# A tridiagonalisation's next row: spread by a transfer and updated in place of a product on TensorE

## The chip, the cores and the metric

The kernel runs on one core of a Trainium2 chip. The metric is the device time of one execution in microseconds (us), the median of three runs. TensorE is called PE in the profile, VectorE DVE, ScalarE ACT, GpSimd POOL and SyncE SP.

## What is computed

The reference passes x (128 graphs of 64 nodes with 256 features, float32) through four graph layers that share one 64 x 64 adjacency matrix:

```python
h = jnp.maximum(_layernorm(x, axis=-1), 0.0)
x = x + _L0_gnn_ref(h, adj, ...)   # two graph products, then LSTMs over windows of 1 to 4 nodes
h = jnp.maximum(_layernorm(x, axis=-1), 0.0)
x = x + _L1_gnn_ref(h, adj, adj, ...)   # Laplacian filter (largest eigenvalue), attention, MLP
h = jnp.maximum(_layernorm(x, axis=-1), 0.0)
x = x + _L2_gnn_ref(h, adj, ...)   # graph attention
h = jnp.maximum(_layernorm(x, axis=-1), 0.0)
x = x + _L3_gnn_ref(h, adj, ...)   # spectral layer
```

The spectral layer needs all eigenvectors of a 64 x 64 symmetric matrix:

```python
L_norm = d_inv_sqrt[:, None] * L * d_inv_sqrt[None, :]
_, U = jnp.linalg.eigh(L_norm)
agg = jnp.einsum('mn,bnd->bmd', U.T, features)
```

The eigenvectors depend on the adjacency matrix alone, so they are found once, while layer 0 runs on the graphs.

## The kernel before

Nothing is issued as it is written. `gnn_kernel` builds a `Plan`, whose proxies for the engines (`V`, `G`, `PE`, `ACT`, `SP`) only record each operation with what it depends on. `Plan.cost` (line 170) gives each one a cost and a latency from a table, `Plan.schedule` (line 221) fills each engine's queue greedily in order of the modelled time, and `Plan.issue` (line 325) writes the queues out. So each engine's order is fixed before the run, and an instruction that is not ready holds up all that stand behind it on its engine. Every instruction is issued from line 331, which is therefore the only line that the profile shows; the groups are told apart by tiles and shapes.

Operations belong to groups. Groups 0 to 7 are layer 0 on an eighth of the graphs each, whose LSTM steps are long runs of float32 matmuls with 256, 336 and 512 columns. Layers 1 to 3 follow in 16 groups of half that size. The eigen solver is a group of its own, `EIG`. `Plan.rank` (line 317) puts its matmuls first and its operations on other engines last among those that can start; a matmul of `EIG` is planned 0.12 us later than the modelled end of what it needs (`slack`). When `EIG` is done, six more buffers of the arena are free for the layers.

`eig_decomp` reduces the matrix to a tridiagonal one with Householder reflections (lines 429 to 485), finds the eigenvalues by bisection, then the vectors, and takes them back with the accumulated reflections. `AQ` (64 x 128) holds the matrix on its left and the accumulated transformation on its right. Every partition keeps its own copy of the row and of the reflection, so that later steps need no spreading. Step k of the reduction does this:

- the row product (line 435): a matmul whose weights are one column of the identity, broadcast, puts row k of the matrix on all partitions, in a PSUM bank (r);
- the reflection: ScalarE squares the row (439), GpSimd takes the root (441), VectorE copies and corrects it to v (443 to 455), and picks each partition's own entry, vc (459);
- the product p (461): a matmul of vc with `AQ`, again on all partitions;
- the row nw (478), its own entry nwc (481), and the rank-2 update of `AQ` by way of a temporary `up` (483 to 485).

The next row product waits for this update. Two more row products after the loop fetch the last diagonal entries.

The lines in the middle of the chain, in short:

```python
PE.matmul(rf[:, :N], idf[:, k:k1].to_broadcast([P, P]), Af, start=True, stop=True)
...
PE.matmul(pf[:, :2 * N], vcf.to_broadcast([P, P]), AQf, start=True, stop=True)
...
V.scalar_tensor_tensor(nw, p, nt, cv, op0=ALU.mult, op1=ALU.add)
```

SyncE's queue carries all transfers but five: the loads of weights and of x, two stores of 1 MB each (`put`) that move the first two eighths of x out after layer 0, their reloads, and the results.

Of the kernel before, what the change touches and what calls it, by code (L numbers as in the profile page):

```python
# [8 lines left out]
ALU = mybir.AluOpType  # L9
# [3 lines left out]
N = 64  # L13
KS = 7
NSWEEP = 9
NEIG = 4080
EPS = 2.0 ** -24

# [315 lines left out]
def eig_decomp(plan, room, adj, adjT, ident, idf, ones):  # L334
# [10 lines left out]

    V, G, PE, ACT = (plan.proxy(e) for e in ("V", "G", "PE", "ACT"))
    kept = {}
    inner = Carver(room.cut(NEIG))  # L350

    def scope():
        inner.reset([0])
        return inner
# [4 lines left out]
    def W(shape, name, bufs=None):  # L359

        if bufs is None:
            bufs = 2 if shape[-1] < N or name == "lab" else 1
        ring = kept.setdefault((name, tuple(shape)), [])
        if len(ring) < bufs:
            ring.append(room.tile(shape))
        else:
            ring.append(ring.pop(0))
        return ring[-1]

    def F(n, name):  # L370

        if name not in kept:
            kept[name] = room.tile([P, n])
            G.memset(kept[name], 0.0)
        return kept[name]

    def PS():
        return plan.value("bank")
# [17 lines left out]
    AQ = AQf[:N]  # L396
# [23 lines left out]
    Af = AQf[:, :N]  # L420
# [3 lines left out]
    V.memset(E[:, N - 1:N], 0.0)  # L424
    ph = scope()
    vb = [ph.tile([N, 2 * N]) for i in range(2)]
    for v in vb:
        G.memset(v, 0.0)
    for k in range(N - 2):
        v = vb[k % 2]  # L430
        k1 = k + 1
        if k >= 2:
            G.memset(v[:, k - 1:k1], 0.0)
        rf = PS()
        PE.matmul(rf[:, :N], idf[:, k:k1].to_broadcast([P, P]), Af, start=True, stop=True)
        r = rf[:N]
        jk = W([N, N], 'junk')
        n2 = W([N, 1], 'n2')
        ACT.activation(jk[:, :N - k1], r[:, k1:N], AF.Square, accum_out=n2)
        s = W([N, 1], 's')  # L440
        G.tensor_tensor(s, n2, half, op=ALU.pow)
        ACT.copy(D[:, k:k1], r[:, k:k1])
        V.tensor_copy(v[:, k1 + 1:N], r[:, k1 + 1:N])
        am = W([N, 1], 'am')
        V.tensor_reduce(am, r[:, k1 + 1:N], op=ALU.max, axis=AX.X, apply_absolute_value=True)
        al = W([N, 1], 'al')
        V.tensor_copy(al, r[:, k1:k1 + 1])
        g = W([N, 1], 'g')
        V.tensor_scalar(g, al, 0.0, -2.0, op0=ALU.is_ge, op1=ALU.mult)
        V.tensor_scalar(am, am, 0.0, None, op0=ALU.is_gt)  # L450
        nz = W([N, 1], 'nz')
        V.scalar_tensor_tensor(nz, n2, 1e-36, am, op0=ALU.is_gt, op1=ALU.mult)
        be = W([N, 1], 'be')
        V.scalar_tensor_tensor(be, g, 1.0, s, op0=ALU.add, op1=ALU.mult)
        V.tensor_sub(v[:, k1:k1 + 1], al, be)
        vcf = F(1, f'vc{k % 2}')
        vc = vcf[:N]
        jk2 = W([N, N], 'junk2')
        V.scalar_tensor_tensor(jk2, v[:, :N], 1.0, ident, op0=ALU.mult, op1=ALU.mult, accum_out=vc)
        pf = PS()  # L460
        PE.matmul(pf[:, :2 * N], vcf.to_broadcast([P, P]), AQf, start=True, stop=True)
        p = pf[:N, :2 * N]
        t1 = W([N, 1], 't1')
        V.scalar_tensor_tensor(t1, al, be, n2, op0=ALU.mult, op1=ALU.subtract)
        V.tensor_scalar(t1, t1, -1e-36, None, op0=ALU.min)
        nt = W([N, 1], 'nt')
        V.reciprocal(nt, t1)
        V.tensor_mul(nt, nt, nz)
        V.scalar_tensor_tensor(E[:, k:k1], v[:, k1:k1 + 1], nz, al, op0=ALU.mult, op1=ALU.subtract, reverse1=True)
        pv = W([N, 1], 'pv')  # L470
        jk3 = W([N, N], 'junk3')
        V.scalar_tensor_tensor(jk3, p[:, :N], 1.0, v[:, :N], op0=ALU.mult, op1=ALU.mult, accum_out=pv)
        c2 = W([N, 1], 'c2')
        V.tensor_scalar(c2, pv, nt, nt, op0=ALU.mult, op1=ALU.mult)
        cv = W([N, 2 * N], 'cv')
        V.tensor_scalar(cv, v, c2, 0.5, op0=ALU.mult, op1=ALU.mult)
        nw = W([N, 2 * N], 'nw')
        V.scalar_tensor_tensor(nw, p, nt, cv, op0=ALU.mult, op1=ALU.add)
        nwc = W([N, 1], 'nwc')
        jk2 = W([N, N], 'junk2')  # L480
        V.scalar_tensor_tensor(jk2, nw[:, :N], 1.0, ident, op0=ALU.mult, op1=ALU.mult, accum_out=nwc)
        up = W([N, 2 * N], 'up')
        V.tensor_scalar(up, nw, vc, None, op0=ALU.mult)
        V.scalar_tensor_tensor(up[:, :N], v[:, :N], nwc, up[:, :N], op0=ALU.mult, op1=ALU.add)
        V.tensor_add(AQ, AQ, up)
    rf = PS()
    PE.matmul(rf[:, :N], idf[:, N - 2:N - 1].to_broadcast([P, P]), Af, start=True, stop=True)
    PE.matmul(rf[:, N:2 * N], idf[:, N - 1:N].to_broadcast([P, P]), Af, start=True, stop=True)
    r = rf[:N]
# [19 lines left out]
    k1 = W([N, N], 'k1')  # L509
# [96 lines left out]
    ph = scope()  # L606
# [3 lines left out]
    SG = ph.tile([N, N + 1, C])  # L610
    for s_ in range(NSWEEP):
        V.tensor_scalar(w, w, 1.0 / (KS + 1), None, op0=ALU.mult)
# [35 lines left out]
    ph = scope()  # L648
# [216 lines left out]
P = 128  # L865
# [46 lines left out]
def gnn_kernel(ctx: ExitStack, tc: tile.TileContext, a, out):  # L912
# [153 lines left out]
    room = Carver(arena)  # L1066

    QT, Vc, inner = eig_decomp(plan, room, adj2[:N], adjT2[:N], ident[:N, :N], ident, ones)
    for dst, lhs, rhs in ((Ublk, QT, Vc), (UTblk, Vc, QT)):
        l2 = inner.tile([P, 2, N])  # L1070
# [491 lines left out]
```

## Time and profile before

| what | value |
|---|---|
| median of 3 runs | 2227.12 us (2226.85 to 2229.72) |
| span of the profiled execution | 2226.0 us |
| PE busy | 2192.1 us, 98% |
| DVE busy | 1682.7 us, 76% |
| ACT busy | 971.0 us, 44% |
| POOL busy | 561.0 us, 25% |
| granted TensorE clock | 0.997 |

The first part of the page gives each engine's busy time and number of instructions. The second cuts the span into 40 slices of 55.65 us and gives the busy share of each in tenths. A busy PE is not PE at its peak, since the matmuls overlap: the distance between the starts of two matmuls tells what one costs. A group's line ends with the idle time of its engine just ahead of it. The list of transfers gives the median time from issue to landing.

### The profile page before, as it was taken

The page shows a single profiled execution, that of the slowest core. Times are in us where ns is not written, and L with a number is a line of the kernel's source. Part 1 is how long each engine was busy: PE and PEld are TensorE (multiplying, and loading weights), DVE is VectorE, ACT ScalarE, POOL GpSimd, SP SyncE. Part 2 cuts the span into 40 slices and gives each one's busy share as a digit, 9 for nine tenths or more (in the row PEclk, how much of TensorE's full clock was granted, in tenths as well). Part 3 has the DMA queues.
Part 4 walks back from the last instruction along what each step waited for, and adds up shares of the span by engine and source line. Part 5 has one row for each costly group of instructions (what it writes and reads, how often), then busy time and mean ns, then how long its engine had stood idle before and what let it go on. Part 6 is the DMA issues. An engine that isn't in the chain of part 4 may idle for free.

```text
span 2226.0 us, 42054 instructions
## 1 busy us (share of the span) xinstructions
PE 2192.1 (98%) x15540; PEld 1507.5 (68%) x15540; DVE 1682.7 (76%) x6966; ACT 971.0 (44%) x1945; POOL 561.0 (25%) x856
## 2 busy tenths in 40 slices
PE   9999999999999999999999999999999999999997
PEld 6568468568558657657647756777777777676776
DVE  7667665755799999999998943467777878776697
ACT  4233343333333333333233343256456566545674
POOL 3101100200100100100100302345545456554353
PEclk9999999999999999999999999999999999999999
DMA  7000000100000000000000011000000000000001
GB/s 256 0 1 20 0 1 1 58 1 1 1 1 1 1 1 1 1 1 1 6 1 1 1 46 33 1 2 1 20 2 20 30 12 30 11 21 1 2 2 58
DMA packets 27694, 36.03 MB, mean 16 GB/s; under 512 B 3552, under 2 KB 24928, under 8 KB 26976
## 3 DMA queue, kind: packets, MB, share of 16 engines
q1 hardware_dynamic: 26384, 32.29, 4.4%
q8 instruction: 122, 2.00, 0.4%
q10 hardware_dynamic: 1104, 1.05, 0.2%
q14 instruction: 84, 0.69, 0.1%
HBM read 22.85 MB, written 10.49 MB: 15 GB/s over the span
## 4 chain that ended last, share of the span: by engine, by line
PE 88%; DVE 8%; ACT 2%; POOL 1%; issue 1%; DMA 0%; SPq 0%; DVEq 0%; ACTq 0%
PE bank L331 88%; DVE arena L331 3%; DVE stat L331 1%; DVE big L331 1%; DVE x L331 1%; DVE mids L331 1%; POOL stat L331 1%; ACT arena L331 1%; ACT mids L331 1%; POOL big L331 0%; ACT big L331 0%; ACT L331 0%; DMA adj<-in_adj_dram 0%; DVE Whh L331 0%; ACT x L331 0%
## 5 line engine op out<-in xcount | busy, mean ns | idle before, releaser
L331 PE MATMUL bank<-big,Wih 128*128 128x256 f32 (+2 forms) x2576 | 859.3, 476 | 5.5 <-ACT big L331 2.1
L331 PEld LDWEIGHTS bank<-big,Wih 128*128 128x128 f32 x2576 | 478.2, 190 | 274.0 <-issue 160.1
L331 ACT ACTIVATE mids<-bank,bl 128x256 f32<-128x256 f32 (+2 forms) x624 | 344.3, 562 | 623.7 <-PE bank L331 615.7
L331 PE MATMUL bank<-big,Whh 128*128 128x256 f32 (+3 forms) x1752 | 505.3, 429 | 0.0
L331 DVE TENSOR_TENSOR arena<-arena 64x21 f32<-64x21 f32 (+6 forms) x2312 | 372.3, 192 | 35.3 <-POOL arena L331 1.7
L331 PEld LDWEIGHTS bank<-big,Whh 128*128 128x128 f32 (+1 forms) x1752 | 306.5, 186 | 132.9 <-issue 66.7
L331 DVE TENSOR_TENSOR big<-big,mids 128x256 f32<-128x256 f32 (+2 forms) x192 | 96.7, 504 | 141.1 <-ACT mids L331 139.8
L331 DVE TENSOR_TENSOR big<-mids 128x512 f32<-128x512 f32 (+2 forms) x256 | 143.3, 563 | 37.6 <-ACT mids L331 34.4
L331 POOL TENSOR_SCALAR stat<-stat 128x4 f32<-128x4 f32 (+1 forms) x228 | 62.6, 275 | 390.3 <-DVE stat L331 377.6
L331 ACT ACTIVATE mids<-big 128x256 f32<-128x256 f32 (+2 forms) x176 | 89.8, 510 | 97.6 <-DVE big L331 68.8
L331 DVE TENSOR_SCALAR arena<-arena 64x1 f32<-64x1 f32 (+5 forms) x596 | 119.2, 208 | 8.9 <-POOL arena L331 0.7
L331 POOL TENSOR_TENSOR big<-big,B1T 128x512 f32<-128x512 f32 x32 | 36.0, 1133 | 349.6 <-DVE big L331 184.6
L331 POOL TENSOR_TENSOR stat<-stat,mhalf 128x4 f32<-128x4 f32 (+1 forms) x114 | 120.4, 1057 | 6.8
L331 POOL TENSOR_TENSOR arena<-arena 64x1 f32<-64x1 f32 x66 | 42.4, 643 | 301.1 <-DVE arena L331 155.4
L331 ACT ACTIVATE mids<-x,stat 128x256 f32<-128x256 f32 x96 | 50.7, 591 | 97.2 <-POOL stat L331 97.1
L331 DVE SCALAR_TENSOR_TENSOR arena<-arena 64x1 f32<-64x1 f32 (+4 forms) x391 | 79.8, 211 | 12.7 <-POOL arena L331 5.5
L331 PE MATMUL bank<-Wih,big 128*128 128x256 f32 (+1 forms) x384 | 87.9, 365 | 0.0
L331 DVE BATCH_NORM_STATS2 stat<-x 128x6 f32<-128x256 f32 x240 | 87.7, 409 | 0.0
L331 PE MATMUL bank<-Whh,big 128*128 128x256 f32 (+1 forms) x400 | 85.4, 357 | 1.9 <-ACT big L331 1.2
L331 POOL MEMSET arena<- 64x2 f32 (+5 forms) x72 | 7.9, 112 | 306.8 <-DVE arena L331 306.8
L331 ACT COPY big<-bank 128x512 f32<-128x512 f32 x86 | 47.2, 585 | 66.2 <-PE bank L331 63.6
L331 PEld LDWEIGHTS bank<-Whh,big 128*128 128x128 f32 (+1 forms) x400 | 62.2, 181 | 19.6 <-issue 7.5
(338 smaller groups left out, 3326.0 us busy)
## 6 DMA issues: line engine op xcount, KB each, us to landing
x<-in_x_dram SPq DMA_DIRECT2D x7, 1024.0 KB, 13.7
out_dram<-x SPq DMA_DIRECT2D x24, 256.0 KB, 2.3
Wih<-in_WihT_dram SPq DMA_DIRECT2D x3, 1024.0 KB, 15.9
Whh<-in_WhhT_dram SPq DMA_DIRECT2D x3, 1024.0 KB, 12.0
put<-x SPq DMA_DIRECT2D x2, 1024.0 KB, 4.4
arena<-put SPq DMA_DIRECT2D x2, 1024.0 KB, 5.1
out_dram<-arena SPq DMA_DIRECT2D x8, 256.0 KB, 2.2
Whh<-in_W_dram SPq DMA_DIRECT2D x2, 512.0 KB, 3.9
```

The lines of the kernel that those rows point to most:

```text
L331: getattr(self.engines[op.eng], name)(*map(real, args), **{k: real(a) for k, a in kw.items()})
```

## The change

From step `KROW` = 6 on there is no row product. Row k + 1 of the old matrix is sent from its partition to all 64 partitions by a transfer at the start of step k (`rb`), while the reflection of step k is computed. When nw is known, two operations on VectorE add the step's update of that row to the copies (`rn`), and step k + 1 reads its row from there, from SBUF. The row does so ahead of the update of `AQ`, which it no longer waits for. The update of `AQ` itself is written as two operations in place, without the temporary. The aim is to take one matmul and its waits out of every step.

```diff
+KROW = 6
...
-    V, G, PE, ACT = (plan.proxy(e) for e in ("V", "G", "PE", "ACT"))
+    V, G, PE, ACT, SP = (plan.proxy(e) for e in ("V", "G", "PE", "ACT", "SP"))
...
     vb = [ph.tile([N, 2 * N]) for i in range(2)]
+    rbs, rns = ([ph.tile([N, N]) for i in range(2)] for j in range(2))
...
-        rf = PS()
-        PE.matmul(rf[:, :N], idf[:, k:k1].to_broadcast([P, P]), Af, start=True, stop=True)
-        r = rf[:N]
+        if k < KROW:
+            rf = PS()
+            PE.matmul(rf[:, :N], idf[:, k:k1].to_broadcast([P, P]), Af, start=True, stop=True)
+            r = rf[:N]
+        else:
+            r = rn
+
+        if k + 1 >= KROW:
+            rb = rbs[k % 2]
+            SP.dma_start(rb[:, k1:], AQ[k1:k1 + 1, k1:N].unsqueeze(1).to_broadcast([1, N, N - k1]))
...
-        up = W([N, 2 * N], 'up')
-        V.tensor_scalar(up, nw, vc, None, op0=ALU.mult)
-        V.scalar_tensor_tensor(up[:, :N], v[:, :N], nwc, up[:, :N], op0=ALU.mult, op1=ALU.add)
-        V.tensor_add(AQ, AQ, up)
+        if k + 1 >= KROW:
+            rn = rns[k % 2]
+            V.scalar_tensor_tensor(rn[:, k1:], nw[:, k1:N], v[:, k1:k1 + 1], rb[:, k1:], op0=ALU.mult, op1=ALU.add)
+            V.scalar_tensor_tensor(rn[:, k1:], v[:, k1:N], nw[:, k1:k1 + 1], rn[:, k1:], op0=ALU.mult, op1=ALU.add)
+        V.scalar_tensor_tensor(AQ, nw, vc, AQ, op0=ALU.mult, op1=ALU.add)
+        V.scalar_tensor_tensor(AQ[:, :N], v[:, :N], nwc, AQ[:, :N], op0=ALU.mult, op1=ALU.add)
```

The built program has 56 matmuls fewer and 57 transfers more on SyncE's queue, and the planner's order changes on every engine.

## The prediction

> **What bounds the kernel now.** I read the page's first two parts, then the chain, then TensorE's own groups and its order of time around one step of the tridiagonalisation, and last the transfers.
>
> ```profile
> PE 2192.1 (98%) x15540; PEld 1507.5 (68%) x15540; DVE 1682.7 (76%) x6966; ACT 971.0 (44%) x1945; POOL 561.0 (25%) x856
> ...
> PE   9999999999999999999999999999999999999997
> ...
> DVE  7667665755799999999998943467777878776697
> ...
> PE 88%; DVE 8%; ACT 2%; POOL 1%; issue 1%; DMA 0%; SPq 0%; DVEq 0%; ACTq 0%
> ```
>
> TensorE is busy in all 40 slices but the last, and the chain that ended last is 88% TensorE. VectorE fills up (slices 13 to 22) only in the bisection. The tridiagonalisation runs from 35 to 604 us, by the first and last row product in the timeline. Windows of it and of the bisection:
>
> ```profile
> 100.00:600.00 500.00, 496.78 (x2540) 335.94 (x2539) 324.79 (x1663) 182.98 (x486) 64.05 (x144) 1.00 0.03 9
> 600.00:1230.00 630.00, 625.77 (x2935) 407.10 (x2934) 580.29 (x2887) 218.69 (x425) 24.97 (x36) 1.00 0.00 1
> ```
>
> The columns are length, then TensorE, weight loads, VectorE, ScalarE, GpSimd. Where the change acts, TensorE has 3.2 us idle in 500 and VectorE is 65% busy. So the eigen chain does not set the time. It is fill-in work, and it costs TensorE the matmuls that it puts between those of layer 0. These are the product p (first line) and the row product (second line, 64 of them, two instructions each):
>
> ```profile
> L331 PE MATMUL bank<-arena 128*128 128x128 f32 x124 | 23.8, 274 | 0.0
> ...
> L331 PE MATMUL bank<-arena,ident 128*128 128x64 f32 x128 | 21.5, 251 | 0.0
> ```
>
> Their last column says that TensorE never idled ahead of them: in the planned order both are ready when their turn comes. What one row product costs is not its 251 ns but how far it pushes the matmuls behind it:
>
> ```profile
> 302.00 1.86 PE L331 MATMUL bank<-big,Wih 128*128 128x336 f32 x6
> 303.70 1.86 PE L331 MATMUL bank<-big,Whh 128*128 128x336 f32 x6
> 305.39 0.33 PE L331 MATMUL bank<-arena,ident 128*128 128x64 f32 x2
> 305.56 0.79 PE L331 MATMUL bank<-big,Whh 128*128 128x336 f32 x2
> 306.18 0.73 PE L331 MATMUL bank<-big,Wih 128*128 128x336 f32 x2
> ```
>
> A 336-column matmul takes (303.70 - 302.00) / 3 = 0.567 us when nothing is between. From the row product's start to the second start behind it, one such matmul included, are 306.18 - 305.39 = 0.79 us. So a row product costs 0.79 - 0.567 = 0.223 us of the bounding engine.
>
> **What the Trainium skill says.** "Perfetto Trace Analysis", section "Identifying the Most-Contended Engine", warns that busy time of matmuls is no measure of distance to the limit because they are pipelined; that is why I price by spacing. The trace agrees: two instructions of 251 ns move the stream by only 223 ns. "DMA: Bandwidth & Descriptors", section "Anatomy of one DMA — SWDGE (gpsimd) path", gives about 2.0 us fixed and bytes / 436e9 on top (for the GpSimd path; ours is SyncE's). The trace's small SyncE transfers land after 2.0 to 2.5 us, which agrees. The same page, "Queues, rings and completion order", says that each DMA engine consumes a ring's descriptors in order; so a row sent behind a 1 MB store waits for it. No row of before shows that.
>
> **The change, part by part.**
>
> *Removed from TensorE:* the row products of steps 6 to 61, 62 - 6 = 56 of them (the built programs hold 8058 and 8002 matmuls). 56 x 0.223 = 12.5 us. Nothing hides it, since the matmuls behind close up.
>
> *Moved:* r is now read from SBUF instead of PSUM, and is made from the copy of the row before the update of AQ instead of after it. The step that this shortens, from the timeline:
>
> ```profile
> 168.18 0.20 ACT L331 ACTIVATE arena<-bank 64x48 f32<-64x48 f32 x1 [0.18 <-PE bank L331]
> ...
> 170.56 0.38 PE L331 MATMUL bank<-arena 128*128 128x128 f32 x2
> ...
> 171.89 0.34 DVE L331 SCALAR_TENSOR_TENSOR arena<-bank,arena 64x128 f32<-64x128 f32 x1
> ...
> 172.41 0.27 DVE L331 TENSOR_SCALAR arena<-arena 64x128 f32<-64x128 f32 x1
> 172.72 0.28 DVE L331 SCALAR_TENSOR_TENSOR arena<-arena 64x64 f32<-64x64 f32 x1
> 173.03 0.28 DVE L331 TENSOR_TENSOR arena<-arena 64x128 f32<-64x128 f32 x1
> ...
> 173.81 0.33 PE L331 MATMUL bank<-arena,ident 128*128 128x64 f32 x2
> ```
>
> From p (170.56) to the end of nw (171.89 + 0.34 = 172.23) are 1.67 us; from the square (168.18) to p 2.38 us; between nw and the next square stood the three updates, the row product and its waking, 173.81 + (168.18 - 167.75, its own row product's start) - 172.23 = 2.0 us. After the change, between nw and the square stand nwc's issue (0.15), two row updates with one AQ update between them (0.27 each after the 64x64 row, the pipelined middle about 0.2) and a wake (0.1): about 1.0 us. The step becomes 1.67 + 1.0 + 2.38 = 5.05 us at most. It may be 4.6 us, since the copies that here alternate with ScalarE on the bank (the idle 0.27 and 0.22 us on VectorE at 168.72 and 169.25) need no turns in SBUF. This shortens a chain that does not bound, so I take nothing for it. The bisection starts and ends earlier, under a TensorE that is full either way.
>
> *On VectorE:* out go tensor_scalar, scalar_tensor_tensor and add (0.27 + 0.28 + 0.28 = 0.83 us), in come four scalar_tensor_tensor (0.34 as the nearest 64x128 one, 0.27, 0.27, 0.27: 1.15 us). 0.3 x 56 = 17 us more on an engine with 175 us idle in this window: hidden.
>
> *Added:* 57 row transfers on SyncE's queue. Nearest rows:
>
> ```profile
> put<-x SPq DMA_DIRECT2D x2, 1024.0 KB, 4.4
> ...
> Whh<-in_L_b_dram SPq DMA_DIRECT2D x1, 64.0 KB, 3.2
> ...
> Whh<-in_g_dram SPq DMA_DIRECT2D x1, 1.0 KB, 2.3
> ```
>
> The last has 256 pieces of 4 bytes; ours has 64 of 8 to 232 bytes. The middle one spreads one row over 128 partitions. So a landing between 2.0 (the skill's fixed part) and 3.2 us; I take 2.4.
>
> *The added wait:* the first row update waits for the landing. Behind it on VectorE, in order, stand the AQ updates and layer 0's gate products; behind those ScalarE's tanh, and p on TensorE, which blocks everything behind it. How much time there is comes from the built program's TensorE order, priced with the trace's spacings (0.43, 0.567 and 0.857 us for 256, 336 and 512 columns, 0.223 us for 64 and 128). Between two p the work was at least 6.05 us before, and is at least 4.96 us after, 5.3 to 5.9 us in most tight steps. From the row update's start to the end of the AQ updates I count 1.0 us, so a landing may take 4.96 - 1.0 = 4.0 us before anything waits. At 2.4, or even 3.2, it is hidden. And a step of 5.05 us against these spacings costs less than 1 us in all (five steps lie below 5.0).
>
> Two rows stand behind the two 1 MB stores in SyncE's order (4.4 us). Each could be late by up to 4.4 + 2.4 - 4.0 = 2.8 us, bounds 0 and 5.6 us together. The planner puts long steps around the stores, so I take 0.
>
> Sum: 2227.1 - 12.5 = 2214.6 us.
>
> **The rivals.**
>
> *A, the stream closes up:* 2214.6 us, give or take 4 us, because the planner recasts the whole order (about 34 us of idle TensorE are spread over the start, the change of layers near 1085 to 1450 us and the last 66 us, where 11.2 are idle). Chance 0.72.
>
> *B, the idle places grow:* the reordered tail, the two stores, or p waiting by some tenths in tight steps give back 8 us: 2222.6 us. Against it: no idle ahead of p now. For it: the tail is decided by near ties in the planner. Chance 0.13.
>
> *C, the idle places shrink:* the eigen solver ends earlier, and its arena becomes buffers for the next layers earlier, which takes some 7 us out of the idle near 1085 to 1450 us: 2207.6 us. Chance 0.08.
>
> *D, the transfer takes the place of the row product:* if a landing took 6 us, a step could not be shorter than 7.0 us, and adding what the steps below that lack gives 40 us: 2214.6 + 40 = 2254 us, slower than before. It breaks even near 5 us (steps of 6.05 us lack 12.7 us). Against it are landings of 2.0 to 3.2 us for small transfers. For it: a row from one SBUF partition to 64 is nowhere in this trace. A VectorE that waits in line would look the same. Chance 0.07.
>
> **How the numbers follow.** The likeliest is A. 2208 to 2223 holds nearly all of A, and half of B and of C: about 0.8. Faster by over 0.2% means below 2222.7 us: A, C and nearly a third of B, 0.84. B's rest gives 0.09 for no change, D 0.07 for slower.
>
> **What would show it.** TensorE's busy time falls by some 10 to 13 us and its idle stays near 34 us. The group of 64-column products with ident shrinks from 128 to 16 instructions. The group of p keeps 0.0 idle ahead of it. Row transfers land in about 2.4 us. The last p comes near 485 us instead of 600 us. I am wrong if VectorE's row update waits for the DMA by a microsecond in most steps, if idle appears ahead of p, or if idle in the last 70 us or at the change of layers moves by more than 5 us.

## The result, and the profile after

The changed kernel took 2206.98 us (2205.22 to 2207.11) beside 2227.37 us (2226.85 to 2229.72) for the kernel before: 20.4 us less, ratio 0.9905, 95% interval 0.9887 to 0.9922. Both times are medians of four runs. The prediction was 2214.6 us with a range of 2208 to 2223. The direction was right, the size was 7.6 us short, and the result lies just below the stated range.

The page of after, busy time first:

```profile
PE 2176.4 (99%) x15428; PEld 1494.9 (68%) x15428; DVE 1689.4 (77%) x7018; ACT 967.3 (44%) x1943; POOL 554.3 (25%) x856
...
PE   9999999999999999999999999999999999999998
...
DVE  7678767769999999999885525468797678776697
...
PE 86%; DVE 9%; POOL 2%; ACT 1%; issue 1%; DMA 0%; SPq 0%; DVEq 0%; ACTq 0%; POOLq 0%
```

TensorE still sets the time. The row of VectorE shows the bisection two slices earlier. TensorE's busy time fell by 15.7 us (2192.1 to 2176.4), and its idle time by 6.9 us: 2226.0 - 2192.1 = 33.9 us of the profiled span before, 2203.4 - 2176.4 = 27.0 us after. The prediction had the first at 10 to 13 us and the second at nothing. (TensorE counts as busy also where its clock is low, so part of a loss can hide in the busy time.)

The same two stretches as in the prediction, in the table of windows (length, then TensorE, weight loads, VectorE, ScalarE, GpSimd, the granted clock, transfers):

```profile
100.00:600.00 500.00, 498.49 (x2473) 331.73 (x2473) 390.22 (x2114) 190.60 (x494) 60.41 (x142) 1.00 0.03 10
600.00:1230.00 630.00, 629.00 (x2955) 419.12 (x2953) 544.29 (x2650) 216.96 (x428) 25.04 (x39) 1.00 0.00 1
```

Idle went from 3.2 to 1.5 us and from 4.2 to 1.0 us, so most of it vanished in and right behind the stretch that the change touches. Here is one step after the change, in the timeline (start, duration, engine, line, what):

```profile
177.57 0.38 PE L332 MATMUL bank<-arena 128*128 128x128 f32 x2
...
179.45 0.34 DVE L332 SCALAR_TENSOR_TENSOR arena<-bank,arena 64x128 f32<-64x128 f32 x1
...
179.98 0.89 DVE L332 SCALAR_TENSOR_TENSOR arena<-arena 64x44 f32<-64x44 f32 x4
...
180.76 0.24 ACT L332 ACTIVATE arena<-arena 64x43 f32<-64x43 f32 x1
...
180.90 0.46 SPq L332 DMA_DIRECT2D arena<-arena  x1
```

The two row updates and the two updates of `AQ` take 0.89 us together (1.0 was counted). The square follows at 180.76, straight from SBUF; the next transfer is issued at 180.90. Of the transfers' view, the longest and a middle row:

```profile
arena<-arena SPq DMA_DIRECT2D x1, 14.5 KB, 2.1
...
arena<-arena SPq DMA_DIRECT2D x1, 7.5 KB, 1.9
```

The 57 transfers landed after 1.9 to 2.8 us, most of them after 1.9 or 2.1 us.

To see where the 20.4 us went I worked a figure out of each trace: for each two successive TensorE instructions, the distance of their starts less the usual distance for that shape (0.216 us for 256 columns, 0.283 for 336, 0.429 for 512, 0.110 for 64 or 128). What is over is called lost time below. It holds idle time, waits inside a run of matmuls and slow stretches. Each figure comes from one profiled execution, and another way of counting the small excesses moves the differences between kernels by up to 1 us. For the 112 removed instructions the usual distances sum to 12.3 us; the lost time fell from 64.9 to 55.6 us, by 9.3. Together this is 21.6 us, near the 22.6 us between the two profiled spans. All that follows is about those 9.3 us.

### The profile page after: what moved, and what is told of

Same layout as the page of the kernel before. It is cut to its first block, busy times and chain, and to the rows that moved or that the text cites. A ratio compares the mean times of both kernels' runs of the same rounds, so it can differ in the third digit from the quotient of the medians.

```text
span 2203.4 us, 42023 instructions
## 1 busy us (share of the span) xinstructions
PE 2176.4 (99%) x15428; PEld 1494.9 (68%) x15428; DVE 1689.4 (77%) x7018; ACT 967.3 (44%) x1943; POOL 554.3 (25%) x856
## 4 chain that ended last, share of the span: by engine, by line
PE 86%; DVE 9%; POOL 2%; ACT 1%; issue 1%; DMA 0%; SPq 0%; DVEq 0%; ACTq 0%; POOLq 0%
PE bank L332 86%; DVE arena L332 3%; DVE stat L332 2%; DVE big L332 2%; DVE x L332 1%; POOL stat L332 1%; DVE mids L332 1%; ACT mids L332 0%; DVE Whh L332 0%; ACT arena L332 0%; ACT big L332 0%; POOL big L332 0%; POOL x L332 0%; ACT x L332 0%; DMA adj<-in_adj_dram 0%
## 5 line engine op out<-in xcount | busy, mean ns | idle before, releaser
L332 PE MATMUL bank<-big,Wih 128*128 128x512 f32 (+2 forms) x2312 | 772.5, 477 | 1.0 <-POOL big L332 0.5
L332 PE MATMUL bank<-big,Whh 128*128 128x256 f32 (+2 forms) x1608 | 495.1, 443 | 2.1 <-DVE big L332 2.1
L332 PEld LDWEIGHTS bank<-big,Whh 128*128 128x128 f32 x1608 | 302.7, 190 | 132.0 <-issue 60.3
L332 DVE TENSOR_TENSOR arena<-arena 64x21 f32<-64x21 f32 (+5 forms) x2255 | 360.1, 191 | 33.0 <-POOL arena L332 1.0
L332 PE MATMUL bank<-arena,Wih 128*128 128x512 f32 (+2 forms) x408 | 146.0, 500 | 0.9 <-DVE Wih L332 0.4
L332 DVE SCALAR_TENSOR_TENSOR arena<-arena 64x1 f32<-64x1 f32 (+15 forms) x567 | 116.2, 229 | 12.7 <-POOL arena L332 6.2
L332 PEld LDWEIGHTS bank<-arena,Wih 128*128 128x128 f32 x408 | 76.3, 190 | 51.4 <-issue 33.7
L332 DVE TENSOR_SCALAR arena<-arena 64x1 f32<-64x1 f32 (+9 forms) x537 | 102.1, 198 | 9.2 <-POOL arena L332 1.0
L332 ACT COPY mids<-bank 128x256 f32<-128x256 f32 (+1 forms) x132 | 57.0, 488 | 78.0 <-PE bank L332 73.7
L332 PE MATMUL bank<-Wg,mids 128*128 128x256 f32 x256 | 64.6, 393 | 0.7 <-ACT mids L332 0.7
```

The lines of the kernel that those rows point to most:

```text
L332: getattr(self.engines[op.eng], name)(*map(real, args), **{k: real(a) for k, a in kw.items()})
```

## The experiments

All times are in us, and each ratio is against runs of the kernel before beside it. The lost time by stretch, for the kernels that the argument rests on:

| | 0-35 | 35-600 | 600-1230 | 1230-1600 | 1600-end | sum |
|---|---|---|---|---|---|---|
| before | 10.5 | 10.2 | 8.8 | 10.7 | 24.7 | 64.9 |
| after | 10.0 | 5.6 | 2.8 | 11.9 | 25.3 | 55.6 |
| a_rowback | 9.9 | 5.7 | 2.7 | 9.8 | 28.9 | 57.0 |
| b_early | 11.2 | 5.6 | 8.5 | 10.3 | 27.3 | 63.0 |
| b_shift40 | 10.6 | 10.2 | 5.7 | 8.0 | 24.7 | 59.3 |
| b_shift40_early | 10.3 | 5.6 | 5.7 | 7.4 | 25.9 | 54.9 |

### The direct price: a_rowback

The kernel after, with 56 row products put back as second product into p's own bank. Nobody reads them, and the order stays.

```diff
+        if k >= KROW:
+            plan.ops[-1].calls.append(("matmul", (pf[:, 2 * N:3 * N], idf[:, k:k1].to_broadcast([P, P]), Af), dict(start=True, stop=True)))
```

> The changed kernel, with the 56 row products put back as work without use: each is issued right behind p, into free columns of p's own bank, outside of the planner's sums, so that the order of every engine stays that of the changed kernel; its output is never read, and the result is the reference's. Theory 1 (a row product costs TensorE 0.223 us, and the rest of the 20 us gained comes from elsewhere): 2207.0 + 56 x 0.223 = 2219.5 us. Rival (the product itself costs more than its spacing tells, and carries the whole gain): 2227 us.

Measured: 2218.99 (2218.71 to 2219.84), ratio 0.9953 (0.9938 to 0.9968). 2218.99 - 2206.98 = 12.0 us, where the prediction had 12.5. The runs of before beside it were 1.3 us slower than those beside the kernel after; by the two ratios the difference is 10.7 us (20.4 - 9.7). So a row product's direct price is 0.19 to 0.21 us, and 8 to 10 of the 20.4 us are not the products' own time.

### One part alone: b_inplace

The kernel before, with only the update of `AQ` made in place.

```diff
-        up = W([N, 2 * N], 'up')
-        V.tensor_scalar(up, nw, vc, None, op0=ALU.mult)
-        V.scalar_tensor_tensor(up[:, :N], v[:, :N], nwc, up[:, :N], op0=ALU.mult, op1=ALU.add)
-        V.tensor_add(AQ, AQ, up)
+        V.scalar_tensor_tensor(AQ, nw, vc, AQ, op0=ALU.mult, op1=ALU.add)
+        V.scalar_tensor_tensor(AQ[:, :N], v[:, :N], nwc, AQ[:, :N], op0=ALU.mult, op1=ALU.add)
```

> The kernel before with one part of the change alone: AQ is updated by two operations in place instead of three by way of a temporary; row products stay. Theory 1: no work leaves TensorE, so 2227 us, give or take what a new order does (3 us). Rival (the shorter chain of the eigen solver is what pays): about 0.3 us x 62 steps of chain, and with it up to 18 us, 2209 us.

Measured: 2228.76, ratio 0.9999 (0.999 to 1.0007). The shorter update by itself brings nothing, as the prediction took it. (The planner made a new order here, too; what it lost near 750 us is told below.)

### The readers of the row's bank: b_pad, b_pick, b_early

The built program tells which PSUM bank each matmul writes. With it I looked in the trace of before for matmuls that start over 0.05 us late into a bank that held a row product until then: ten of them lose 3.5 us, all between 35 and 600 us. Nine of the ten stand between 100 and 600 us and lose 3.0 us. The kernel after has one, at 67 us, ahead of step 6. (The expectations below rest on a coarser count: eight at 3.9 us, and 4.7 us in before and 1.8 us in after with the solver's other banks.) One of the nine, in the timeline of before:

```profile
206.26 0.33 PE L331 MATMUL bank<-arena,ident 128*128 128x64 f32 x2
...
206.63 0.19 DVE L331 COPY arena<-bank 64x41 f32<-64x41 f32 x1 [0.88 <-PE bank L331]
206.94 0.20 ACT L331 ACTIVATE arena<-bank 64x42 f32<-64x42 f32 x1 [5.37 <-DVE arena L331]
...
207.26 0.19 DVE L331 TENSOR_REDUCE arena<-bank 64x1 f32<-64x41 f32 x1 [0.44 <-ACT arena L331]
...
207.48 0.15 ACT L331 COPY arena<-bank 64x1 f32<-64x1 f32 x1 [0.26 <-DVE arena L331]
...
207.67 0.15 DVE L331 COPY arena<-bank 64x1 f32<-64x1 f32 x1 [0.22 <-ACT arena L331]
...
207.87 0.70 PE L331 MATMUL bank<-big,Wih 128*128 128x256 f32 x2 [0.36 <-DVE arena L331]
```

The five readers of the bank take turns: VectorE copies, ScalarE squares, VectorE reduces, ScalarE copies into D, VectorE copies al, each with an idle that the other engine ends. So the bank is given back 1.2 us after the product's end (207.82 - 206.59), and a layer-0 matmul that the plan has put into this bank waits. That readers on two engines take turns agrees with the Trainium skill, "PSUM — Partial Sum Buffer", section "PSUM bank collisions raise a hardware error": the compiler adds a dependency between instructions on different engines that touch one bank, reads included. The plan does not know of these turns: `Plan.record` notes a dependency only where one of two operations writes, so its model can give the bank back too early. In the waits of this stretch (35 to 600 us) VectorE's on ScalarE over the arena are 24.0 us in 78 places before, and 3.1 us in 8 after.

Two attempts to take these stalls out of the kernel before missed. b_pad lets the plan take an eigen bank as free 0.8 us later:

```diff
-                    free[v.kind][v.buf] = v.done
+                    free[v.kind][v.buf] = v.done + (0.8 if v.kind == "bank" and v.group == self.aside else 0.0)
```

> The kernel before, whose planner takes a PSUM bank that the eigen solver used as free 0.8 us later than modelled, so that no other matmul is put on it before its last reader is done; row products stay. Theory 1a (in before, some matmuls of layer 0 wait for a bank that the row product held, 3.9 us in all): these waits are gone, 2227.4 - 3.9 = 2223.5 us. Rival (what the change gained beyond the row products is a chance of the new order): the time moves either way by up to 5 us, with no link to these waits, and the waits on the row product's bank were not lost time.

Measured: 2228.9, ratio 0.9999 (0.999 to 1.0008). The stalls fell from 3.5 to 0.8 us and the lost time between 35 and 600 us from 10.2 to 6.9, but the plan also ordered the rest anew and lost as much behind 1460 us. Inconclusive. The same edit on the kernel after (a_pad):

> The changed kernel with the same later release of the eigen solver's banks in the planner. Theory 1a: the changed kernel has no matmul of layer 0 that waits for such a bank, so there is nothing to gain: 2207 us, give or take 3 us for a new order. Rival (the later release helps by itself): 2203 us as well as before minus 4.

Measured: 2209.15, ratio 0.9907 (0.9892 to 0.9922): nothing gained. b_pick keeps before's order and only prefers, among free banks, one that the eigen solver has not just given back:

```diff
-                    v.buf = min(f, key=lambda i: (f[i], i))
+                    if v.kind == "bank":
+                        v.buf = min((i for i in f if f[i] <= t), key=lambda i: (pref.get(i, 0.0), i))
```

> The kernel before, every instruction in its place on every engine; only which of the free PSUM banks a tile takes is chosen differently: a bank that the eigen solver has just given back is taken last. If the stalls behind late readers of a row product's bank are part of the unforeseen gain (the trace of before shows 4.7 us of them, 3.9 us in the stretch from 100 to 600 us), the time falls by 2.9 to 3.9 us, to about 2224 us, and those stalls go from the trace. The rival, that such short stalls are given back later in the stream: 2227 us as before.

> Both cures in the kernel before: the bisection later by about 40 us (63 more GpSimd instructions, as in the run that shifted it alone, 2221.7 us) and the banks picked as in the run that does it alone. If the two losses are separate and add, 2221.7 - 2.9 = 2218.8 us, which is what the kernel after with its row products put back took (2219.0 us): then the two losses together are the whole unforeseen part of the gain. If the losses are one and the same, or the banks are worth nothing: 2222 us.

Measured: 2227.77, ratio 1.0002 (0.9994 to 1.0011), and 2221.97, 0.9972 (0.9962 to 0.9981). No effect, but the cause wasn't taken away: in b_pick the stalls are still there, 4.3 us of them. At the nine larger ones the built program has six or all of the other seven banks in use, so there is hardly another bank to take.

b_early takes the readers off the bank instead. VectorE's first reader copies the whole row to SBUF; VectorE's others read that, and the copy into D moves from ScalarE to VectorE. Only ScalarE's square still reads the bank. TensorE's instructions, order and banks stay as they are.

```diff
+        if k >= 6:
+            rs = rss[k % 2]
+            plan.ops[-2].calls = []
+            plan.ops[-1].calls = [("tensor_copy", (rs[:, k:], r[:, k:N]), {}), ("tensor_copy", (v[:, k1 + 1:N], rs[:, k1 + 1:]), {})]
...
+            plan.ops[-1].calls = [("tensor_copy", (al, rs[:, k1:k1 + 1]), {}), ("tensor_copy", (D[:, k:k1], rs[:, k:k1]), {})]
```

> The kernel before with TensorE's instructions, their order and their banks unchanged; from step 6 on VectorE first copies the row from PSUM to SBUF, and the other readers on VectorE and the copy into D read that, so that the row's bank is given back by the first of VectorE's readers and not by the third, or by ScalarE's copy. If the stalls behind those late readers set part of the time (eight of them in 100 to 600 us, 3.9 us), most of them go, and the stretch and the whole time fall by 2 to 4 us, to about 2225 us. The rival, that such stalls are given back at once or later: 2228 us, as before. Two more short VectorE instructions per step lie on a chain with room.

Measured: 2223.87 beside 2228.52, ratio 0.9979 (0.997 to 0.9988): 4.7 us faster (2.7 to 6.7 by the interval), with two instructions per step more on VectorE. The stalls fell from 3.5 to 0.1 us, and the lost time between 35 and 600 us from 10.2 to 5.6, the value of after. The place shown above, in the timeline of b_early:

```profile
204.65 0.33 PE L331 MATMUL bank<-arena,ident 128*128 128x64 f32 x2
...
205.02 0.20 DVE L331 COPY arena<-bank 64x43 f32<-64x43 f32 x1 [0.88 <-PE bank L331]
205.25 0.18 DVE L331 COPY arena<-arena 64x41 f32<-64x41 f32 x1
205.33 0.20 ACT L331 ACTIVATE arena<-bank 64x42 f32<-64x42 f32 x1 [5.79 <-DVE arena L331]
...
205.74 0.64 PE L331 MATMUL bank<-big,Wih 128*128 128x256 f32 x2
```

From the row product to the layer-0 matmul are 1.09 us now, 1.61 us before (207.87 - 206.26). TensorE's order is the same throughout, and the gain lies in the stretch of the row products. This cause is shown.

### The end of a bisection sweep: b_shift40, a_shift24

Behind 600 us the largest loss of before stands at 1082 us. Its timeline, VectorE and TensorE:

```profile
1076.39 0.86 DVE L331 TENSOR_SCALAR arena<-arena 64x1365 f32<-64x1365 f32 x1
...
1077.85 1.54 DVE L331 TENSOR_TENSOR arena<-arena 64x1344 f32<-64x1344 f32 x1
...
1079.43 3.08 DVE L331 TENSOR_REDUCE arena<-arena 64x21 f32<-64x1344 f32 x1
...
1082.44 2.46 DVE L331 TENSOR_TENSOR x<-x,bank 128x512 f32<-128x512 f32 x4
1084.83 1.27 DVE L331 TENSOR_TENSOR mids<-bank,nB 128x512 f32<-128x512 f32 x2
1085.56 1.52 PE L331 MATMUL bank<-adjTb,mids 64*64 64x64 f32 x64 [2.90 <-DVE mids L331]
```

The matmuls that TensorE has to run meanwhile:

```profile
1075.98 2.32 PE L331 MATMUL bank<-Wg,mids 128*128 128x256 f32 x10
1078.13 1.93 PE L331 MATMUL bank<-ident,big 128*128 128x128 f32 x16
1079.90 0.60 PE L331 MATMUL bank<-Wg,mids 128*128 128x256 f32 x2
1080.43 1.16 PE L331 MATMUL bank<-adjTb,mids 64*64 64x64 f32 x64
1081.52 1.13 PE L331 MATMUL bank<-Wg,mids 128*128 128x256 f32 x4
```

The last three operations of a sweep, 5.5 us of VectorE, fall onto the change of layer 0 from one eighth to the next, where TensorE needs VectorE's results at once. The additions into x wait behind the reduce, and TensorE, which has run out of other matmuls, stands still for 2.9 us. Then it is slow; the last but one column of the windows is its granted clock:

```profile
1087.00:1088.00 1.00, 0.94 (x10) 0.34 (x3) 1.00 (x4) 0.00 (x0) 0.00 (x0) 0.70 0.00 0
1088.00:1089.00 1.00, 1.00 (x3) 0.48 (x2) 1.00 (x4) 0.00 (x0) 0.00 (x0) 0.50 0.00 0
1089.00:1090.00 1.00, 1.00 (x3) 0.48 (x2) 0.73 (x3) 0.00 (x0) 0.00 (x0) 0.50 0.00 0
1090.00:1091.00 1.00, 1.00 (x2) 0.34 (x2) 0.24 (x1) 0.00 (x0) 0.00 (x0) 0.60 0.00 0
```

The missing clock sums to 0.30 + 0.50 + 0.50 + 0.40 = 1.7 us. The same pause of 2.9 us stands in b_early, b_pad and b_pick. In the kernel after, the bisection ends some 110 us earlier, its last reduce of 3.08 us starts at 1036.75, and the same change of layer 0 at 1064.76 shows an idle of 0.38 us:

```profile
1064.76 1.52 PE L332 MATMUL bank<-adjTb,mids 64*64 64x64 f32 x64 [0.38 <-DVE mids L332]
```

So of the pause and the slow clock, 4.6 us in before, 0.4 us is left. To move the bisection, b_shift40 puts 63 dependent GpSimd operations ahead of it in the kernel before. They make a value that changes nothing. The plan leaves TensorE's order as it was up to 608 us and makes a new one behind it.

```diff
+    zz = W([N, 1], 'zz')
+    V.tensor_scalar(zz, AQ[:, 0:1], 0.0, 1.0, op0=ALU.mult, op1=ALU.add)
+    for i in range(63):
+        G.tensor_tensor(zz, zz, half, op=ALU.pow)
+    V.scalar_tensor_tensor(E[:, N - 1:N], zz, 0.0, E[:, N - 1:N], op0=ALU.mult, op1=ALU.add)
```

> The kernel before with 63 such roots, a shift of the bisection by about 40 us. Theory 2: the sweep's end at 1079 us leaves the change at 1075 to 1087 us, whose 5 us of idle TensorE go, and none of the other sweeps' ends (763, 833, 887, 940, 1010, 1065, 1119) falls on a change: about 2223 us. Rival (the idle time belongs to the row products or to the change of layers itself): 2227 us, with as much idle there as before.

Measured: 2221.72 (2221.02 to 2223.1), ratio 0.9968 (0.9955 to 0.998): 6.3 us faster with the eigen solver *later*. But the sweeps' ends didn't leave the change. The bisection moved by 51 us (its first reduce from 670.18 to 720.96), which is about one sweep, so that the end of the sweep before now lies there. Its reduce starts 1.8 us earlier than the other did in before, it has 2.75 us of matmuls beside it (in before, ten of those instructions ran ahead of the reduce, at 1075.98), and the idle is 0.35 us:

```profile
1077.63 3.07 DVE L331 TENSOR_REDUCE arena<-arena 64x21 f32<-64x1344 f32 x1
...
1078.61 2.75 PE L331 MATMUL bank<-Wg,mids 128*128 128x256 f32 x12
1080.63 2.46 DVE L331 TENSOR_TENSOR x<-x,bank 128x512 f32<-128x512 f32 x4
...
1083.87 1.52 PE L331 MATMUL bank<-adjTb,mids 64*64 64x64 f32 x64 [0.35 <-DVE mids L331]
```

Between 600 and 1230 us 3.1 us are won, and 2.7 us more between 1230 and 1600, where the vectors' part of the solver lies otherwise too. So the pause went with a sweep's end still at the change: how the plan orders TensorE's work there matters too, and this run doesn't part that from where the sweep ends. What eases the later stretch is open. The reverse, a_shift24, pushes the bisection of the kernel after back towards the change, with 38 such operations:

> The changed kernel with 38 roots of 1.0 in line on GpSimd (0.6 us each) between the tridiagonalisation and the bisection, which shift the bisection by about 24 us against layer 0; GpSimd is idle there, and the result stays the reference's. Theory 2 (the change gained some 5 us because the end of a bisection sweep, 5.5 us of long VectorE instructions, no longer falls on the change from one eighth of layer 0 to the next): the sweep's end that comes at 1037 us moves to about 1061 us, onto the change at 1058 to 1066 us; TensorE's idle time around it grows by 3 to 5 us and the time to about 2211 us. Rival (no link between the two; the idle time of before came from the row products): no more idle time there, 2207 us.

Measured: 2210.24 (2208.96 to 2212.13), ratio 0.9918 (0.9903 to 0.9933): 3.3 us slower than after, though the two intervals overlap. The sweep's end came onto the change as aimed, but the pause of 3 to 5 us did not:

```profile
1061.38 3.07 DVE L332 TENSOR_REDUCE arena<-arena 64x21 f32<-64x1344 f32 x1
...
1062.36 2.76 PE L332 MATMUL bank<-Wg,mids 128*128 128x256 f32 x12
1064.38 2.46 DVE L332 TENSOR_TENSOR x<-x,bank 128x512 f32<-128x512 f32 x4
...
1067.62 1.52 PE L332 MATMUL bank<-adjTb,mids 64*64 64x64 f32 x64 [0.35 <-DVE mids L332]
```

Here, too, the plan has twelve matmul instructions, 2.76 us, beside the reduce. The lost time between 600 and 1230 us went from 2.8 to 6.6, in other places (1.2 us at 1077, 0.9 us at 1182 and smaller ones). So the pause of before is read from its trace, and it is gone in the kernel after; that the place of a sweep's end alone makes it is not shown. What the two runs show is that shifting the solver, with the new order that the plan makes for it, moves the time by 3 to 6 us.

### Both together: b_shift40_early

> The same early copy of the row together with the bisection moved later by about 40 us, so that neither loss is left in the kernel before. If the two losses add and are all of the unforeseen gain: 2221.8 - 2.8 = 2219 us, the time of the kernel after with its row products put back. The rival: 2222 us, and 3 us of the gain have another cause.

Measured: 2216.84 (2216.13 to 2217.53), ratio 0.9946 (0.9934 to 0.9959). The gains add: 4.7 + 6.3 = 11.0, and 11.7 us were measured. The kernel before, with all its row products, is now where the kernel after with its row products stands (ratio 0.9953, 0.9938 to 0.9968). The sums agree (54.9 us of lost time here, 55.6 us in the kernel after), but not all in the same places: between 35 and 600 us both lose 5.6 us; between 600 and 1230 us it is 5.7 us here and 2.8 us in the kernel after; behind 1230 us it is 33.3 us (7.4 + 25.9) here and 37.2 us (11.9 + 25.3) there. So the first gain is the same one, and the second only in part.

### How much room the landing had: a_dma2, a_dma3

The kernel after with the row passed through one or two more SBUF copies, each a transfer of its own (three in a row shown). The order stays.

```diff
+            rq = rqs[k % 2]
+            plan.ops[-1].calls = [("dma_start", (rq[0][:, k1:], AQ[k1:k1 + 1, k1:N].unsqueeze(1).to_broadcast([1, N, N - k1])), {}), ("dma_start", (rq[1][:, k1:], rq[0][:, k1:]), {}), ("dma_start", (rb[:, k1:], rq[1][:, k1:]), {})]
```

> The changed kernel with two transfers in line for each row (row to all partitions, then those copies to the place where they are read), every engine's order unchanged; the result is the reference's. A landing took 2.1 us, so the pair takes about 4.4. Theory 1 (the wait for the landing has about 4.0 us of room in the tightest step): a step can't be shorter than 4.4 + 1.0 = 5.4 us, the steps below that lack 3 us together, 2207 + 3 = 2210 us. Rival (the row transfer already bounds the step, and its time is what the step's length is made of): 2.2 us more in some 35 tight steps, 2284 us at most, 2250 at least.

> The same with three transfers in line, some 6.6 us. Theory 1: a step can't be shorter than 7.6 us; by the spacings of TensorE's order the steps below that lack 61 us together, 2207 + 61 = 2268 us. Rival (room much larger than 4 us, since the order is seldom tight on the chip): below 2220 us.

Measured: two in a row land after 3.6 us (median, 3.5 to 5.7), and the time is 2208.24, ratio 0.9907 (0.9892 to 0.9922), the 1.3 us being about the runs' scatter. Three land after 5.5 us (5.2 to 7.4), and the time is 2226.73, ratio 0.9994 (0.9985 to 1.0003): the whole gain is gone. VectorE's waits in a_dma3:

```profile
DVE arena L332 <- DMA arena<-arena: 40.3, 36, 2.9
```

These are 40.3 us in 36 waits; the kernel after has no such line. So the room lies between 3.6 and 5.5 us, which fits the 4.0 us worked out, and the rival with a slow transfer was right in kind. The expected 2268 us missed since each further transfer adds some 1.8 us, not the 2.2 us that I took: with 5.5 + 1.0 = 6.5 us as the shortest step, what the steps below that lack sums to 23.8 us by the distances between the starts of p in the trace of after, and 19.7 us were measured.

### Other first steps: a_krow2_pick, a_krow34

`KROW = 2` with b_pick's choice of banks, and `KROW = 34`.

> The kernel after with the row transfer from step 2 on in place of step 6 (four more row products gone, 4 x 0.223 = 0.9 us) and the banks picked so that one just given back by the eigen solver is taken last (1.8 us of such stalls are left in the kernel after, about 1 us of it can go). Expected 2207 - 0.9 - 1.0 = 2205 us; the planner makes a new order from step 2 on, which has moved the time by up to 4 us either way in other runs: 2201 to 2209 us. The rival, that early rows wait for their transfer because the stores of the first steps share the queue: 2209 us or more.

> The kernel after with the row transfer from step 34 on in place of step 6: 28 row products come back. At 0.223 us each the time is 2207 + 6.2 = 2213.2 us; with the waits behind the readers of their banks (up to 2.5 us in the half of the stretch where they stood) up to 2216 us. The planner makes a new order, and the end of the bisection moves later by the 28 longer steps: if a sweep end falls on a change of layer 0 again, up to 5 us more. The rival, that the row products cost only their own time: 2213 us.

Measured: 2210.12 (2207.99 to 2214.39), ratio 0.9924 (0.9909 to 0.9939), no better than after; its new order, in the profiled execution, which was the slowest of the four, loses 4 us more in the first 35 us and 3.7 us more between 600 and 1230 us. And for `KROW = 34` 2217.73 (2216.53 to 2219.32), ratio 0.9956 (0.9941 to 0.9971), for 28 row products kept: 10.7 us more than after, of which some 6 are the products and 3.4 the lost time between 35 and 600 us, where seven stalls behind row products, 3.1 us, are back. That is 0.38 us per row product, well over its own 0.19 to 0.21 us. None of these kernels beats the one after.

## Why the prediction was wrong by 7.6 us

Right, by its steps:

- *The bound.* TensorE in all 40 slices, before and after.
- *Removed: 56 x 0.223 = 12.5 us.* Measured 10.7 to 12.0 us.
- *The landing, 2.4 us taken of 2.0 to 3.2.* 1.9 to 2.8 us, hidden; the room of 4.0 us is bracketed: a landing of 3.6 us cost next to nothing, one of 5.5 us 19.7 us.
- *The stores taken as 0, p with 0.0 idle ahead, the last p near 485 us.* The two rows behind the stores are issued 9 to 10 us after them, when the stores have landed (3.9 and 4.0 us), so that no row had to wait for one. The group of p in after still shows 0.0 idle, no row update waits for a landing, and the last p is at 485.1 us.

```profile
L332 PE MATMUL bank<-arena 128*128 128x128 f32 x124 | 24.2, 277 | 0.0
```

- *VectorE +17 us, hidden.* Hidden, and only +6.7 us (1682.7 to 1689.4).

Wrong is the step *Moved*, at the sentence "This shortens a chain that does not bound, so I take nothing for it", and with it the forecast that TensorE's "idle stays near 34 us" (27.0 us were left). Two terms were left out of the sum:

1. *The row's PSUM bank, 4.7 us, shown by b_early.* The prediction saw the readers take turns on the bank, and saw that the change ends it. It asked what this does to the eigen chain, which has room. It did not ask who takes the bank next. It also took the 0.0 idle ahead of the row product and p as a sign that nothing waits: a wait that an instruction causes shows at the one that follows in its buffer, mostly a layer-0 matmul from the group of `Wih`.
2. *The pause at the end of a sweep, some 4 us of the 6.0 us won between 600 and 1230 us.* The prediction said that the bisection "starts and ends earlier, under a TensorE that is full either way". The last but one sweep of before cost TensorE 2.9 us of idle and then 1.7 us of clock. A move by 110 us could have been to a worse place as well: in b_inplace two of a sweep's long operations (0.86 and 1.55 us, from 743.0 to 745.4) lie right ahead of another change of layer 0, and TensorE idles 0.63 and 1.97 us behind them, the clock falls again, and some 5 us are lost from 747 to 757 us. So this term is luck in its sign, and belonged into the range; it could not have been taken as a gain from the edit alone. Whether it was the place of the sweep's end or the plan's new order around it that removed the pause stays open.

By the lost time, 4.6 us were won between 35 and 600 us and 6.0 between 600 and 1230; behind 1230 us the kernel after gives 1.8 us back.

Rival C, idle that shrinks, came closest with 2207.6 us, but not by its reason. It had the solver end earlier and buffers come free earlier near 1085 to 1450 us. TensorE's idle time in that stretch was 5.2 us before and is 3.3 us after, 1.9 us less and not 7, and the lost time between 1230 and 1600 us rose from 10.7 to 11.9. b_shift40, where the solver ends later, loses *less* there (8.0). Its 0.08 was too low because it had been tied to that one reason.

## What to carry to other kernels

When an instruction leaves a full engine, its price is its own spacing and also what its output buffer does: list the readers of that buffer, which engines they alternate on, and the next writer of the same buffer, above all where all buffers are in use. A background task with a few long operations on a shared in-order engine has a phase against the main work; two edits that moved it by tens of microseconds moved the time by 3 to 6 us here, one in each direction. So give it a place in the range, and look at where the long operations come to lie and at what work the plan leaves beside them. And to test a cause in a planned kernel, keep the plan and change only the cause: b_early did; b_pad, b_shift40 and a_shift24 didn't, and their totals mix the cause with a new order.

## What the runs showed of the hardware

A pause of TensorE can cost more than its length. After the 2.9 us at 1082 us the granted clock was down to 0.50 for 3.4 us, 1.7 us lost on top; the same happened in b_inplace near 752 us, and in b_early, b_pad, a_krow2_pick and a_shift24 after pauses of 1.2 to 2.9 us, near 1083 us or between 1380 and 1910 us. It doesn't follow every such pause: the kernel after has one of 2.1 us at 1380 us without it. In slices of 2 us the kernel before shows it once between 40 us and its last 2 us, and the kernel after never. The Trainium skill, "TensorE: Matmul & The Clock Gate", section "What's actually happening", has the array at half rate until about 3.4 us of sustained work, in a window that doesn't follow the kernel; the length of the dips here, and their coming and going, agree. It has the clock drop after an idle window of about 3.4 us; here pauses of 1.2 to 2.9 us were enough, and the measurement decides.

A row of 2 to 58 floats from one SBUF partition to 64 landed 1.9 to 2.8 us after its issue on SyncE's queue, mostly 1.9 or 2.1 us, and each copy that waits for the one before it added some 1.8 us.
